# State space layer: one scan over two states from a zero start, the first token's state put into dt x B beforehand

## The chip, the cores and the metric

The kernel runs on one core of a Trainium2 chip. The core's engines work side by side, each through its own list of instructions in order: TensorE (PE; its weight loads are listed as PEld), VectorE (DVE), ScalarE (ACT), GpSimd (POOL), and SyncE (SP), which issues the DMAs. An instruction waits on semaphores until its inputs are there, and everything behind it on its engine waits with it. The metric is the device time of one execution in microseconds (us), smaller being better. All data is float32.

## The reference

Two layers, each added to its input: `x = x + L0(gn(x))`, then `x = x + L1(gn(x))`, on x of shape 4 x 384 x 64 x 64. L1 is attention over 7 x 7 windows and is the same in both kernels. L0 is a state space layer over the 4096 tokens of an image. For each of 768 inner channels d and 16 states n:

```python
dt  = softplus(dt_low @ dt_w.T + dt_b)      # per token and channel
A   = -exp(A_log)
def step(h, inp):
    dt_t, B_t, C_t, x_t = inp
    dA  = exp(dt_t[:, :, None] * A[None])
    dBx = (dt_t * x_t)[:, :, None] * B_t[:, None, :]
    h   = dA * h + dBx                        # the recurrence over tokens, h starts at 0
    y_t = einsum('bdn,bn->bd', h, C_t)
    return h, y_t
```

Around it: a group norm and a layer norm, an input projection to xb and a gate z, a causal convolution of 4 taps with SiLU on xb (the result is xc), the projections that give dt_low, B and C, and at the end `y + xc * D`, times SiLU(z), through the output projection.

## The kernel before, in words

Layer 0 runs in 64 steps: 4 images of 16 chunks of T = 256 tokens. The 768 channels are ND = 6 tiles d of 128 partitions. A tile's 16 states are four groups of NG = 4, so a step has 24 units m = 4 d + g. Each unit is worked in two slots, one for each half (two states), so that a step has 48 slots. What follows happens for one unit:

- `driven` (L595) makes db = (dt x) times B for four states in one instruction of 128 x 1024, on VectorE or on GpSimd. The table `AT['driven']` (L298) gives for each m its slot and a 1 for VectorE, 0 for GpSimd: before, 14 go to VectorE and 10 to GpSimd. VectorE reads dt x from a copy in PSUM (`dtx_ps`, copied by ScalarE in `dt_x_copied`, L592), GpSimd from SBUF. db has six buffers.
- `decay` (L605) makes da = exp(dt A) on ScalarE, one instruction of 128 x 256 for each state, into a PSUM tile of two states. Two of these tiles exist, so ScalarE can be one half ahead of VectorE: the decays of slot s + 1 are issued in slot s, and their tile comes free when the scans of slot s - 1 have ended.
- `scans` (L616) runs the recurrence on VectorE, one scan of 128 x 256 for each state, which starts from `state` (from 0.0 in the first chunk of an image). The result is hs, which has five buffers.
- `kept_states` (L629) copies the last token's states from hs into `state` on ScalarE, one copy of 128 x 4 for each unit, in the slot after the unit.
- `with_c` (L633) multiplies hs by C in place on GpSimd, one instruction of 128 x 1024 for each unit.
- `summed` (L637) adds the 16 states by transposing matmuls into PSUM (one buffer, `y`). For each pair of tiles d, `turn` (L654) copies that out on ScalarE, turns it back on TensorE and gates it on VectorE.

The order around this is written by hand. Every other piece of work has a slot in the table `AT` (L287), counted from the first slot of its step; negative slots lie in the step before and slots from 48 on in the step after. Within a slot, the ScalarE pieces come in this order: first decay, `kept_states` in even slots, second decay, and then the others; `with_c` and the scans follow, and then the other pieces on the other engines. The engines keep exactly this order. The pieces of one step that are prepared in the step before are the convolution and the projections (`prepared`, L425), whose `burst` (L479) runs all SiLUs between two loads of the activation table, the softplus (`softplus`, L514: three pairs of tiles, each a chain of projection, absolute value and relu, exp, plus one, ln, correction on VectorE, sum on TensorE, copy) and the layer norm (`normed`, L352). `rows` (L493) writes B and C to DRAM and reads each group of four states back into all 128 partitions, eight DMAs of 512 KB for each step on SP's queue; the four B tiles and four C tiles have one buffer for each group, which comes free when the last user in the step before has ended.

Layer 1 (from L821) starts when layer 0 has ended and isn't touched.

Of the kernel before, what the change touches and what calls it, by code (L numbers as in the profile page):

```python
# [8 lines left out]
F32 = mybir.dt.float32  # L9
# [39 lines left out]
def two_layers(  # L49
# [223 lines left out]
    def layer0(x1s, mvs, gms1):  # L273

        with ExitStack() as es:
            es.enter_context(tc.manual_schedule(engines=in_step))
            ps_a = es.enter_context(tc.tile_pool(name="ps_a", bufs=2, space=PSUM))
            ps_x = es.enter_context(tc.tile_pool(name="ps_x", bufs=1, space=PSUM))
# [8 lines left out]
            AT = {  # L287
             'norm': (9, 20, 21, 22, 22, 25, 28, 30, 32, 33, 33),
             'kept': -11,
             'x': ((-9, -8, -4, -4), (-6, -6, -3, -2), (-4, -4, -1, 1)),  # L290
             'c': ((1, 1, 5, 6), (3, 4, 8, 8), (8, 9, 13, 13)),
             'z': ((8, 9, 13, 13), (10, 11, 15, 15), (14, 15, 19, 21)),
             'burst': (25, 26, 28, 31),
             'softplus': ((32, 34, 36, 36, 37, 38, 40, 42), (34, 38, 39, 40, 42, 43, 44, 48),
                          (45, 49, 50, 50, 51, 51, 52, 55)),
             'dtx': (-5, -1, 8, 17, 19, 33),
             'dtx_ps': (-3, 4, 13, 20, 24, 36),
             'driven': ((-5, 0), (-2, 1), (-1, 1), (1, 1), (1, 0), (5, 1), (7, 0), (7, 1),  # L298
                        (11, 0), (14, 1), (14, 0), (16, 1), (19, 0), (21, 1), (23, 0), (25, 1),
                        (25, 1), (25, 1), (29, 0), (32, 1), (34, 0), (38, 1), (39, 0),  # L300
                        (41, 1)),
             'turn': (21, 25, 26),
             'out': (8, 17, 18, 19, 20, 22, 23, 27, 29, 30),
            }
            ACT = 1
            dtx_ps = ps_x.tile([P, 2, T], F32, name="dtx_ps")
            def group_norm(b, mv):
# [117 lines left out]
            def prepared(I, h, at):  # L425
# [67 lines left out]
                def rows():  # L493

                    xd = h["xd"] = w1.tile([NX, T], F32, tag="xd", name=f"xd_{b}_{i}")
                    nc.scalar.copy(xd, h["pd"][:NX, 0, :])
                    rows = dram.tile([2 * NS, T], F32, tag="bcrows", name=f"bcrows_{b}_{i}")
                    nc.sync.dma_start(rows, xd[DTR:NX, :])
                    h["B"], h["C"] = [], []
                    for tag in "BBBBCCCC":  # L500
                        g = len(h[tag])
                        t = bc.tile([P, NG, T], F32, tag=tag, name=f"{tag}_{b}_{i}_{g}")
                        r0 = g * NG + (NS if tag == "C" else 0)
                        src = rows[r0 : r0 + NG, :]
                        nc.sync.dma_start(t, src.unsqueeze(0).broadcast_to([P, NG, T]))
                        h[tag].append(t)
# [7 lines left out]
                def softplus(q, slots):  # L514
# [53 lines left out]
                    at(next(n), project)  # L568
                    s = next(n)
                    for k in range(2):  # L570
                        at(s, lambda k=k: part("e", AF.Abs, k), ACT)
                        at(s, lambda k=k: part("r", AF.Relu, k), ACT)
# [9 lines left out]

            dbs, das = {}, {}

# [7 lines left out]
            def dt_x_copied(d, h):  # L592
                nc.scalar.copy(dtx_ps[:, d % 2, :], h["dtx"][d])  # L593

            def driven(I, m, h, eng):  # L595

                d, g = divmod(m, NS // NG)
                db = w2.tile([P, NG, T], F32, tag="db", name=f"db_{I}_{m}", bufs=6)
                dtx = dtx_ps[:, d % 2, :] if eng is nc.vector else h["dtx"][d]
                eng.tensor_tensor(  # L600
                    db, dtx.unsqueeze(1).broadcast_to([P, NG, T]), h["B"][g], ALU.mult
                )
                dbs[I, m] = db

            def decay(I, m, half, k, h):  # L605

                d, g = divmod(m, NS // NG)
                n = g * NG + 2 * half + k
                if k == 0:
                    das[I, m, half] = ps_a.tile([P, 2, T], F32, tag="da", name="da")  # L610
                act(
                    das[I, m, half][:, k, :], h["dt"][d // 2][:, d % 2, :], AF.Exp,
                    scale=nega[:, d, n : n + 1],
                )

            def scans(I, m, half, hs):  # L616

                d, g = divmod(m, NS // NG)
                da = das.pop((I, m, half))
                for k in range(2):  # L620
                    j = 2 * half + k
                    n = g * NG + j
                    nc.vector.tensor_tensor_scan(  # L623
                        hs[:, j, :], da[:, k, :], dbs[I, m][:, j, :],
                        state[:, d, n : n + 1] if I % NCHUNK else 0.0,
                        ALU.mult, ALU.add,
                    )

# [117 lines left out]
            for I in range(STEPS):  # L746
# [7 lines left out]
                for d in range(ND):  # L754
                    at(AT["dtx"][d], lambda I=I, d=d, h=h: dt_x(I, d, h))
                    at(AT["dtx_ps"][d], lambda d=d, h=h: dt_x_copied(d, h), ACT)
                for m, (slot, vector) in enumerate(AT["driven"]):
                    eng = nc.vector if vector else nc.gpsimd
                    at(slot, lambda I=I, m=m, h=h, eng=eng: driven(I, m, h, eng))
                if I % NCHUNK == 0 and I + NCHUNK < STEPS:  # L760
                    next_batch(I // NCHUNK, slot_of(I))
# [461 lines left out]
```

## Time and profile before

| | us |
|---|---|
| median of 5 runs (8261.52 to 8269.91) | 8268.89 |
| profiled execution, its own time | 8266.53 |
| span of the profile | 8264.5 |
| layer 0, from the start to the last copy of states (5918.1) | 5918 |
| of it one step, from the copies of states (120.2 to 5918.1, 64 steps) | 90.65 |

Busy time between 1000 and 5000 us of the span, all inside layer 0:

| engine | busy, us of 4000 | us of one step of 90.65 |
|---|---|---|
| VectorE | 3767.8 | 85.4 |
| GpSimd | 3663.5 | 83.0 |
| TensorE | 3615.4 | 81.9 |
| ScalarE | 3245.9 | 73.6 |

The second column is the first divided by 4000 and multiplied by 90.65. Busy time counts a stretch in which two instructions of an engine overlap once. VectorE and ScalarE overlap the end of one instruction with the start of the next, so a row of many instructions takes less than their number times the mean of one; what an instruction adds to such a row is read from the timeline.

### The profile page before, as it was taken

The numbers are of one execution on the slowest core, as the hardware profiler recorded it, in microseconds if no ns is written. First come the engines' busy times: TensorE is split into PE (matmuls) and PEld (weight loads), VectorE is DVE, ScalarE is ACT, GpSimd is POOL, SyncE is SP. The second block draws the span as 40 slices with busy tenths as digits, with TensorE's granted clock in tenths as the row PEclk, the third lists the DMA queues.
The fourth block names the chain that finished last, engine by engine and source line by source line (L and its number), as shares of the span: only waits on it lengthen the run. The fifth ranks groups of instructions, "written<-read, shape, count | busy, mean of one in ns | idle before, by whom it ended". The sixth has DMA issues, their size and how long they took to land. (4 is left out here: it accounts for less than half of the span.)

```text
span 8264.5 us, 144369 instructions
## 1 busy us (share of the span) xinstructions
PE 7504.8 (91%) x48570; PEld 5811.4 (70%) x48570; DVE 6989.0 (85%) x12725; ACT 5890.5 (71%) x15613; POOL 6982.7 (84%) x4247
## 2 busy tenths in 40 slices
PE   7988998899899989988998999899799999999999
PEld 6777777777777777777777777777555555555555
DVE  5999999999999999999999999999666666666666
ACT  5888887888888887888878888888455455455455
POOL 4999998989999999999999999999677777677777
PEclk9999999999999999999999999999899999999999
DMA  3112211221121112112211211121223233232322
GB/s 111 62 61 72 70 59 59 67 67 60 64 76 62 55 62 75 60 64 73 66 53 59 66 60 55 60 71 51 80 84 87 85 89 88 82 88 84 89 82 64
DMA packets 327528, 583.40 MB, mean 71 GB/s; under 512 B 62940, under 2 KB 211180, under 8 KB 326660
## 3 DMA queue, kind: packets, MB, share of 16 engines
q1 hardware_dynamic: 326788, 574.17, 22.3%
q8 instruction: 387, 6.34, 0.3%
q14 instruction: 353, 2.89, 0.1%
HBM read 471.49 MB, written 84.73 MB: 67 GB/s over the span
## 5 line engine op out<-in xcount | busy, mean ns | idle before, releaser
L635 POOL TENSOR_TENSOR hs<-hs,C 128x1024 f32<-128x1024 f32 x1536 | 3615.8, 2362 | 468.9 <-ACT state L631 451.5
L623 DVE TENSOR_TENSOR_SCAN hs<-da,state,db 128x256 f32<-128x256 f32 x5760 | 3850.4, 730 | 121.1 <-issue 90.8
L96 ACT ACTIVATE da<-dt,nega 128x256 f32<-128x256 f32 x6144 | 2892.0, 475 | 885.1 <-DVE hs L623 839.7
L648 PE MATMUL y<-ident,hs 128*128 128x128 f32 x12288 | 1729.9, 293 | 596.6 <-POOL hs L635 355.2
L999 POOL TENSOR_SCALAR sg<-sg,rsum 128x308 f32<-128x308 f32 x1536 | 1618.8, 1072 | 641.7 <-DVE rsum L997 630.6
L648 PEld LDWEIGHTS y<-ident,hs 128*128 128x128 f32 x12288 | 1516.3, 151 | 892.7 <-POOL hs L635 518.3
L600 POOL TENSOR_TENSOR db<-dtx,B 128x1024 f32<-128x1024 f32 x640 | 1513.8, 2365 | 5.1
L409 PE MATMUL mm_ps<-xn,w_in 128*128 128x256 f32 x4608 | 1120.5, 390 | 2.0 <-DVE xn L380 1.9
L600 DVE TENSOR_TENSOR db<-dtx_ps,B 128x1024 f32<-128x1024 f32 x896 | 1065.6, 1201 | 0.7 <-ACT dtx_ps L593 0.7
L96 ACT ACTIVATE sg<-sg,mx 128x308 f32<-128x308 f32 x1536 | 828.6, 541 | 250.7 <-DVE mx L984 231.2
L984 DVE CUSTOM_DVE_ANT_0 sg<-lg_ps,bias 128x308 f32<-128x308 f32 x1536 | 643.1, 475 | 381.1 <-PE lg_ps L978 381.1
L409 PEld LDWEIGHTS mm_ps<-xn,w_in 128*128 128x128 f32 x4608 | 883.1, 198 | 114.9 <-DVE xn L380 2.7
L416 PE MATMUL mm_ps<-xb,dcv 128*128 128x256 f32 x3072 | 715.6, 379 | 0.0
L1027 ACT COPY tb<-pt_ps 88x512 f32<-88x512 f32 x384 | 221.8, 578 | 625.3 <-PE pt_ps L1023 625.2
L416 PEld LDWEIGHTS mm_ps<-xb,dcv 128*128 128x128 f32 x3072 | 571.7, 189 | 75.7 <-issue 0.3
L695 PE MATMUL mm_ps<-yg,w_out 128*128 128x256 f32 x2304 | 553.8, 381 | 0.0
L1014 DVE COPY ta<-pt_ps 110x512 f32<-110x512 f32 x768 | 492.5, 683 | 23.2 <-PE pt_ps L1009 23.2
L695 PEld LDWEIGHTS mm_ps<-yg,w_out 128*128 128x128 f32 x2304 | 437.1, 192 | 58.5
L1009 PE MATMUL pt_ps<-ident,sg 128*110 128x128 f32 x3072 | 417.7, 279 | 0.8 <-POOL sg L999 0.8
L1009 PEld LDWEIGHTS pt_ps<-ident,sg 128*110 128x110 f32 x3072 | 322.7, 133 | 77.9 <-issue 48.4
L882 PE MATMUL mm_ps<-xn,w_qkv 128*128 128x512 f32 (+2 forms) x612 | 278.0, 592 | 60.5 <-DVE xn L869 53.3
L978 PE MATMUL lg_ps<-k,q 32*128 32x308 f32 x3072 | 311.2, 473 | 0.0
(149 smaller groups left out, 10011.4 us busy)
## 6 DMA issues: line engine op xcount, KB each, us to landing
B<-bcrows SPq DMA_DIRECT2D x256, 512.0 KB
C<-bcrows SPq DMA_DIRECT2D x256, 512.0 KB
vw<-vd SPq DMA_DIRECT2D x1792, 33.0 KB
xr<-x SPq DMA_DIRECT2D x28, 1056.0 KB
vd<-v SPq DMA_DIRECT2D x280, 96.0 KB
xi<-in_x_dram SPq DMA_DIRECT2D x64, 384.0 KB
xo<-in_x_dram SPq DMA_DIRECT2D x64, 384.0 KB
x<-xo SPq DMA_DIRECT2D x64, 384.0 KB
```

Source lines behind the costliest of these rows:

```text
L96: ins = nc.scalar.activation(o, i, func, **kw)
L409: nc.tensor.matmul(pb[:, k, :], w_in[:, j, m * P : (m + 1) * P], xn[:, j, :], start=(j == 0), stop=(j == NJ - 1),)
L416: nc.tensor.matmul(pb[:, k, :], dcv[:, d, c, :], xb[:, d, c : c + T], start=(c == 0), stop=(c == KC - 1),)
L600: eng.tensor_tensor(db, dtx.unsqueeze(1).broadcast_to([P, NG, T]), h["B"][g], ALU.mult)
L623: nc.vector.tensor_tensor_scan(hs[:, j, :], da[:, k, :], dbs[I, m][:, j, :], state[:, d, n : n + 1] if I % NCHUNK else 0.0, ALU.mult, ALU.add,
L635: nc.gpsimd.tensor_tensor(hs, hs, h["C"][m % (NS // NG)], ALU.mult)
L648: nc.tensor.matmul(y[:, d % 2, half, :], hs[:, k, half * P : (half + 1) * P], ident, is_transpose=True, start=(first and half == 0 and d % ...
L695: nc.tensor.matmul(po, w_out[:, d, m * P : (m + 1) * P], h["yg"][d // 2][:, d % 2, :], start=False, stop=(d == ND - 1),)
L984: nc.vector.tensor_tensor_reduce(sg[:, hh, :], lg[:, :NK], bias[:, 4 * m + hh, :], -1.0, BIG, ALU.add, ALU.min, mx[:, hh : hh + 1],)
L999: nc.gpsimd.tensor_scalar(sg[:, hh, :], sg[:, hh, :], rs[:, hh : hh + 1], None, ALU.mult)
L1009: nc.tensor.transpose(pt[: KN[c], col : col + P], sg[:, 2 * pair + hh, KOFF[c] : KOFF[c] + KN[c]], ident,)
L1014: nc.vector.tensor_copy(t[: KN[0], :, :].rearrange("p a q -> p (a q)"), pt[: KN[0], :])
```

## The change

Two states are scanned by one instruction of 128 x 512 that starts from zero. At the border between the two, the decay is zero, which is how the second state begins afresh: the two PSUM tiles of decays are now fixed (`da_ps`), their first column of each state is set to zero once at the start, and `decay` writes only the other 255 columns. The state carried from the chunk before enters through db: its first column of each state gets the whole state of the first token, dA h + dBx. For that:

- a small DMA in `rows` brings the first token's B for 16 states into all 128 partitions (`B0`, 128 x 16);
- `start_decay` makes the first token's decays on ScalarE (six of 128 x 16 a step, none in the first chunk of an image);
- `first_states` makes the first token's states on GpSimd (a multiply by the first dt x, and, except in the first chunk, a multiply by the kept states and an add; 128 x 16 each, six tiles d);
- `begun` copies four of them into the first column of db on ScalarE (24 copies of 128 x 4 a step);
- `driven` writes the other 255 columns of each state. 16 of the 24 go to VectorE and 8 to GpSimd.

The table of slots is written anew throughout. Softplus has one more slot, so that its two pairs of absolute value and relu lie in slots of their own, and its third pair of tiles lies in slots 57 to 69, inside the step that uses it.

```diff
-            ps_a = es.enter_context(tc.tile_pool(name="ps_a", bufs=2, space=PSUM))
+            ps_a = es.enter_context(tc.tile_pool(name="ps_a", bufs=1, space=PSUM))
...
             AT = {
-             'norm': (9, 20, 21, 22, 22, 25, 28, 30, 32, 33, 33),
-             'kept': -11,
-             'x': ((-9, -8, -4, -4), (-6, -6, -3, -2), (-4, -4, -1, 1)),
-             'c': ((1, 1, 5, 6), (3, 4, 8, 8), (8, 9, 13, 13)),
-             'z': ((8, 9, 13, 13), (10, 11, 15, 15), (14, 15, 19, 21)),
-             'burst': (25, 26, 28, 31),
-             'softplus': ((32, 34, 36, 36, 37, 38, 40, 42), (34, 38, 39, 40, 42, 43, 44, 48),
-                          (45, 49, 50, 50, 51, 51, 52, 55)),
-             'dtx': (-5, -1, 8, 17, 19, 33),
-             'dtx_ps': (-3, 4, 13, 20, 24, 36),
-             'driven': ((-5, 0), (-2, 1), (-1, 1), (1, 1), (1, 0), (5, 1), (7, 0), (7, 1),
-                        (11, 0), (14, 1), (14, 0), (16, 1), (19, 0), (21, 1), (23, 0), (25, 1),
-                        (25, 1), (25, 1), (29, 0), (32, 1), (34, 0), (38, 1), (39, 0),
+             'norm': (11, 19, 19, 20, 20, 22, 26, 26, 30, 30, 32),
+             'kept': -15,
+             'x': ((-11, -11, -8, -7), (-11, -11, -7, -5), (-7, -6, -4, -3)),
+             'c': ((-3, -2, 0, 5), (3, 3, 7, 8), (15, 16, 18, 19)),
+             'z': ((1, 2, 3, 5), (10, 11, 14, 15), (8, 15, 16, 18)),
+             'burst': (25, 28, 28, 31),
+             'softplus': ((31, 33, 34, 36, 36, 37, 39, 39, 42),
+                          (44, 47, 47, 50, 50, 51, 52, 52, 55),
+                          (57, 60, 61, 61, 63, 65, 66, 66, 69)),
+             'dtx': (-5, -3, 9, 13, 23, 29),
+             'dtx_ps': (-3, 5, 10, 17, 24, 31),
+             'driven': ((-4, 0), (-3, 1), (-1, 1), (-1, 1), (1, 0), (6, 0), (6, 1), (8, 1),
+                        (10, 1), (11, 1), (14, 1), (15, 1), (18, 0), (19, 1), (23, 0), (25, 1),
+                        (25, 0), (26, 1), (30, 0), (32, 1), (35, 1), (36, 0), (36, 1),
                         (41, 1)),
-             'turn': (21, 25, 26),
-             'out': (8, 17, 18, 19, 20, 22, 23, 27, 29, 30),
+             'turn': (21, 24, 26),
+             'out': (11, 17, 21, 23, 23, 24, 26, 27, 29, 30),
+             'e0': (-4, -2, 11, 12, 23, 26),
+             'h0': (-4, -1, 11, 16, 24, 32),
+             'first': (-3, 0, 0, 4, 3, 7, 9, 10, 13, 14, 19, 18, 23, 23, 25, 27, 29, 30, 32, 33,
+                       38, 41, 41, 46),
             }
             ACT = 1
+            da_ps = [ps_a.tile([P, 2, T], F32, name=f"da_{half}") for half in range(2)]
+            for t in da_ps:
+                nc.vector.memset(t[:, :, 0:1], 0.0)
...
                     nc.sync.dma_start(rows, xd[DTR:NX, :])
+                    h["B0"] = small.tile([P, NS], F32, tag="b0", name=f"b0_{b}_{i}")
+                    with nc.allow_non_contiguous_dma(reason="one token"):
+                        nc.sync.dma_start(
+                            h["B0"],
+                            rows[:NS, 0:1].rearrange("n t -> t n").broadcast_to([P, NS]),
+                        )
...
                     at(next(n), project)
-                    s = next(n)
                     for k in range(2):
+                        s = next(n)
                         at(s, lambda k=k: part("e", AF.Abs, k), ACT)
                         at(s, lambda k=k: part("r", AF.Relu, k), ACT)
...
+            def start_decay(d, h):
+                h["e0", d] = w2.tile([P, NS], F32, tag="e0", name=f"e0_{d}", bufs=ND)
+                act(
+                    h["e0", d], nega[:, d, :], AF.Exp, scale=h["dt"][d // 2][:, d % 2, 0:1]
+                )
+
+            def first_states(I, d, h):
+                h["h0", d] = w2.tile([P, NS], F32, tag="h0", name=f"h0_{d}", bufs=ND)
+                dtx = h["dtx"][d][:, 0:1]
+                nc.gpsimd.tensor_scalar(h["h0", d], h["B0"], dtx, None, ALU.mult)
+                if I % NCHUNK:
+                    nc.gpsimd.tensor_tensor(h["e0", d], h["e0", d], state[:, d, :], ALU.mult)
+                    nc.gpsimd.tensor_tensor(h["h0", d], h["h0", d], h["e0", d], ALU.add)
+
+            def begun(I, m, h):
+                d, g = divmod(m, NS // NG)
+                nc.scalar.copy(dbs[I, m][:, :, 0], h["h0", d][:, g * NG : (g + 1) * NG])
...
                 eng.tensor_tensor(
-                    db, dtx.unsqueeze(1).broadcast_to([P, NG, T]), h["B"][g], ALU.mult
+                    db[:, :, 1:], dtx[:, 1:].unsqueeze(1).broadcast_to([P, NG, T - 1]),
+                    h["B"][g][:, :, 1:], ALU.mult,
                 )
...
-                if k == 0:
-                    das[I, m, half] = ps_a.tile([P, 2, T], F32, tag="da", name="da")
                 act(
-                    das[I, m, half][:, k, :], h["dt"][d // 2][:, d % 2, :], AF.Exp,
+                    da_ps[half][:, k, 1:], h["dt"][d // 2][:, d % 2, 1:], AF.Exp,
                     scale=nega[:, d, n : n + 1],
                 )
...
             def scans(I, m, half, hs):
-                d, g = divmod(m, NS // NG)
-                da = das.pop((I, m, half))
-                for k in range(2):
-                    j = 2 * half + k
-                    n = g * NG + j
-                    nc.vector.tensor_tensor_scan(
-                        hs[:, j, :], da[:, k, :], dbs[I, m][:, j, :],
-                        state[:, d, n : n + 1] if I % NCHUNK else 0.0,
-                        ALU.mult, ALU.add,
-                    )
+                pair = slice(2 * half, 2 * half + 2)
+                nc.vector.tensor_tensor_scan(
+                    hs[:, pair, :].rearrange("p k t -> p (k t)"),
+                    da_ps[half].rearrange("p k t -> p (k t)"),
+                    dbs[I, m][:, pair, :].rearrange("p k t -> p (k t)"),
+                    0.0, ALU.mult, ALU.add,
+                )
...
+                    if I % NCHUNK:
+                        at(AT["e0"][d], lambda d=d, h=h: start_decay(d, h), ACT)
+                    at(AT["h0"][d], lambda I=I, d=d, h=h: first_states(I, d, h))
                 for m, (slot, vector) in enumerate(AT["driven"]):
...
+                    at(AT["first"][m], lambda I=I, m=m, h=h: begun(I, m, h), ACT)
```

## The prediction

> **What bounds the kernel now.** I read the page first: its slices say where each engine is full, its groups what fills it.
>
> ```profile
> span 8264.5 us, 144369 instructions
> ...
> PE   7988998899899989988998999899799999999999
> ...
> DVE  5999999999999999999999999999666666666666
> ACT  5888887888888887888878888888455455455455
> POOL 4999998989999999999999999999677777677777
> ...
> L635 POOL TENSOR_TENSOR hs<-hs,C 128x1024 f32<-128x1024 f32 x1536 | 3615.8, 2362 | 468.9 <-ACT state L631 451.5
> L623 DVE TENSOR_TENSOR_SCAN hs<-da,state,db 128x256 f32<-128x256 f32 x5760 | 3850.4, 730 | 121.1 <-issue 90.8
> ```
>
> Slices 2 to 28 are layer 0; no slice there has an engine at rest. Then the busy time inside layer 0, by windows (length; busy and count of PE, PEld, DVE, ACT, POOL; clock, DMA):
>
> ```profile
> 1000.00:2000.00 1000.00, 904.88 (x4982) 769.52 (x4980) 942.09 (x1360) 809.63 (x2061) 914.23 (x449) 0.94 0.19 64
> 2000.00:3000.00 1000.00, 899.20 (x4974) 765.77 (x4974) 947.35 (x1356) 814.03 (x2071) 918.16 (x452) 0.94 0.20 64
> ```
>
> With the two windows that follow, a step of 90.65 us holds 85.4 us of VectorE, 83.0 of GpSimd, 81.9 of TensorE and 73.6 of ScalarE. VectorE is the bound, but GpSimd is 2.4 us and TensorE 3.5 us below it: what VectorE sheds beyond that another engine keeps. VectorE rests 5.2 us a step. The waits from 1000 to 5000 us, 44.1 steps, say for what:
>
> ```profile
> ACT da L96 <- DVE hs L623: 576.4, 785, 3.1
> ...
> POOL hs L635 <- ACT state L631: 316.8, 362, 3.9
> ...
> DVE yg L678 <- PE mm_ps L671: 115.1, 104, 2.9
> ...
> DVE hs L623 <- issue: 66.9, 89, 1.2
> ```
>
> VectorE waits 2.6 us a step for TensorE's gated sums and 1.5 with no releaser shown. ScalarE and GpSimd wait for VectorE's scans (13.1 and, through the kept states, 7.2 us). So VectorE sets the pace and the others follow it.
>
> **The change, part by part.** Durations are those of the profiled execution, 8266.53 us (2.4 us under the median of the five runs; span 8264.5).
>
> *Scans.* The timeline gives what one more scan costs in a row of them; the price of a moved product stands beside it.
>
> ```profile
> 130.47 8.54 DVE L623 TENSOR_TENSOR_SCAN hs<-da,db 128x256 f32<-128x256 f32 x14
> ...
> 2053.70 6.70 DVE L623 TENSOR_TENSOR_SCAN hs<-da,state,db 128x256 f32<-128x256 f32 x10
> ...
> 2066.59 3.46 DVE L600 TENSOR_TENSOR db<-dtx_ps,B 128x1024 f32<-128x1024 f32 x3
> ```
>
> From zero, one scan alone takes 0.671 us in its group and 14 take 8.54: (8.54 - 0.671)/13 = 0.605 each. From a kept state, (6.70 - 0.730)/9 = 0.663. No row has 512 columns. VectorE's statistics of 256 and 512 elements take 407 and 669 ns, so 145 ns of such an instruction don't depend on its length. Taken off the scan alone that leaves 0.526 us for 256 columns, and a scan of 512 in a row costs 0.605 + 0.526 = 1.13. [...]
>
> A pair from kept states goes from 1.326 to 1.13, 0.195 less, 9.4 us for 48 halves; in the 4 first chunks from 1.21 to 1.13, 3.8 us. Mean over 64 steps: 9.0 us less.
>
> *Products.* VectorE gets 16 instead of 14, each 1.13 us by the row of three above: 2.3 us more. GpSimd gets 8 instead of 10 at 2.33 us (2.365, less the overlap that rows of them show): 4.7 less. [...]
>
> VectorE: 85.4 - 9.0 + 2.3 = 78.7.
>
> *First token on GpSimd.* 18 instructions of 128 x 16 a step. Its product of 256 takes 731 ns and of 1024 2362 ns, which leaves 0.22 us for 16 elements; a fill of one element takes 0.1, the pad copy of 18 elements 0.2. So 1.8 to 4.5 us; I take 3.7. GpSimd: 83.0 - 4.7 + 3.7 = 82.0.
>
> *Copies and decays on ScalarE.* The copy of kept states has the shape of `begun`: 0.184 us alone, but in the timeline the next instruction starts 0.10 us after it.
>
> ```profile
> 2061.93 0.19 ACT L631 COPY state<-hs 128x4 f32<-128x4 f32 x1
> 2062.03 0.48 ACT L96 ACTIVATE da<-dt,nega 128x256 f32<-128x256 f32 x1
> ...
> 2066.43 1.28 ACT L96 ACT_TABLE_LOAD   x1
> 2067.72 1.67 ACT L96 ACTIVATE xc<-xc 128x512 f32<-128x512 f32 x3
> 2069.30 1.66 ACT L96 ACTIVATE sz<-sz 128x512 f32<-128x512 f32 x3
> 2070.97 1.28 ACT L100 ACT_TABLE_LOAD   x1
> ```
>
> 24 copies: 2.4 us, 4.4 at most. Six small exps at 0.2 (the exp of 32 x 1) to 0.28 (that of 128 x 96): 1.1 us after overlap. `kept_states` stays. ScalarE: 77.1, at most 79.7.
>
> *The B0 load.* One DMA of 2048 elements behind `bcrows` on SP, ahead of the B tiles. SP waits there anyway: 33 us a step for buffers that GpSimd and VectorE free (662.2, 509.7 and 277.1 us over 44 steps).
>
> ```profile
> SPq L505 <- POOL hs L635: 662.2, 176, 6.7
> SPq L505 <- POOL db L600: 509.7, 87, 10.0
> ...
> SPq L505 <- DVE db L600: 277.1, 87, 7.4
> ```
>
> In the step shown `bcrows` goes out at 2079.77 and the first B at 2090.34: 10 us of cover. Nearest row: the 25 loads of 784 runs of 28 bytes, issued in 16.06 us, 0.64 each; three times that is 1.7 us. I cost it nothing; without cover it would hold the first h0 by 2 us. [...] B's last tile has six slots from its last reader to its next instead of eight, still over 10 us. The fills of da_ps: once, 0.2 us.
>
> *Order.* Softplus lies in slots 31 to 69 instead of 32 to 55 and has the same instructions. Three places turn bad; each is the sum of what stands in a slot.
> - Burst, slots 25 and 26. ScalarE needs 0.8 (decays), then 5.84 (2066.43 to 2072.27), then 0.9 for the next decays: 7.6 us. VectorE had three products, a normalisation, two pairs of scans, gate and statistics to do meanwhile, 7.9 us. Now it has two scans, two products, gate and statistics: 5.4. It rests 2.2 us.
> - First unit, slots -4 and -3. `first_states` stands on GpSimd behind a `with_c` that starts 0.65 us after slot 44's start and takes 2.36; its copy on ScalarE is in slot 45, so the decays of slot 47, issued behind it, start 3.6 us (with 0.6 for h0) after the scan of slot 43 instead of 2.3 to 2.4: 1.2 us.
> - Slots 0 to 5. ScalarE: twelve decays at 0.41 (their distance in the timeline) 4.9, four copies of 256 columns with a bias 1.5, four steps of 512 columns 2.1, three copies of states, four of `begun` and one of dt x 1.0: 9.5. VectorE: six scans, a correction, half a statistic, 7.7, and 1.1 that it is behind from slot 47 (three and a half us of scan and products there, ScalarE 2.3). It rests 0.7 us.
>
> *Sum.* A step: 90.65 - 85.4 + 78.7 = 84.0 with the rest as today, + 2.2 + 1.2 + 0.7 = 88.1. 64 steps save 64 x 2.6 = 166 us: 8266.5 - 166 = **8100 us**. GpSimd would be busy 82.0 of 88.1, 93%, no more than VectorE is now (94%).
>
> **Rivals.**
> - *ScalarE held by `begun`: slower.* ScalarE runs in order, so a copy whose h0, or whose whole db, GpSimd still owes holds all decays behind it. For it: four copies follow within two slots a GpSimd product that stands behind a `with_c` (m = 0, 4, 5, 18), and ScalarE has 3.5 us a step less to give away. Against it: copy and product write different elements, so only h0 need be waited for, and h0 is early in five tiles of six. If the copy does wait for the product: first unit 3.6 instead of 1.2, m = 5 2.7 us, m = 4 and 18 some 1.4 each, 7.9 in all, some 5 after what VectorE has in hand: a step of 93, 64 x 2.35 = 150 more than before, 8417. It decides from 2.6 us a step on.
> - *The scan of 512 costs twice the 256: slower too.* VectorE sheds 5.2 us (5.6 in 60 steps of 64) instead of 9.0: a step of 91.9, 80 us more, 8347. Against it the fixed 145 ns.
> - *GpSimd takes the pace.* Its 82.0 plus the 7.2 it waits for states today is 89.2; 64 x 1.45 = 93 us less: 8174.
> - *No new stalls.* The spread softplus covers the three places. 84.0 would have GpSimd busy for 98%; at 96% it is 85.4: 8266.5 - 64 x 5.25 = 7930.
>
> **How the numbers follow.** My forecast 0.40, no new stalls 0.14, GpSimd's pace 0.12, held ScalarE 0.23, the dear scan 0.07, and 0.04 for a tie of gain and stalls. What a measurement here can tell from no change is 0.2%, 17 us. Faster 0.40 + 0.14 + 0.12 = 0.66, same 0.04, slower 0.30. The forecast's own range is 8020 to 8180. The whole range reaches down to 7910, just past the case without stalls, and up to 8400, short of the held ScalarE's 8417: about 0.07 lies below and 0.13 above.
>
> **What would show it.** Right: scans of 128 x 512 at about 1.2 us each; VectorE's share in layer 0 at 89 to 90% and its waits for ScalarE's da, now 18 us in 44 steps, above 100; GpSimd's wait for states smaller; nothing waiting for B0. Wrong: scans at 1.3 or more; long ScalarE waits for GpSimd's h0 or db; a GpSimd small operation above 0.3 us; TensorE waiting longer for GpSimd's hs (220.9 us in 44 steps now), which would keep hs buffers and stop the scans.

## The result, and the profile after

The changed kernel takes 8285.19 us (median), the kernel before 8267.61: a ratio of 1.0023, with a 95% interval of 1.0017 to 1.0028. It is a little slower. The forecast was 8100 us.

The page after shows the same slices and groups as before. VectorE's slices went from 9 to 8, and ScalarE's are at 8 without a gap.

```profile
span 8283.8 us, 144249 instructions
...
PE   6898999899989889998989899899799999999999
...
DVE  5888888888888888888888888888666666666666
ACT  4888888888888888888888888888555455455455
POOL 3999998989999898999989899999677777677777
...
L656 DVE TENSOR_TENSOR_SCAN hs<-da,db 128x512 f32<-128x512 f32 x3072 | 3622.8, 1211 | 355.7 <-ACT da L96 209.3
```

The scan of 512 takes 1.211 us and all scans together 3622.8 us instead of 4085.8 (3850.4 and the 235.4 of the first chunks). So VectorE did shed the work. The windows inside layer 0 (length; busy and count of PE, PEld, DVE, ACT, POOL; clock, DMA) say the same:

```profile
1000.00:2000.00 1000.00, 899.99 (x4968) 760.27 (x4966) 886.62 (x851) 839.72 (x2377) 905.23 (x613) 0.96 0.21 63
2000.00:3000.00 1000.00, 899.64 (x4965) 759.19 (x4962) 888.58 (x850) 844.35 (x2394) 912.63 (x627) 0.96 0.21 64
```

Copies of states now run from 128.3 to 5934.6 us, so a step takes 90.78 us instead of 90.65. The span is 19.3 us longer: 8.1 before the first copy of states, 8.4 in the steps, 2.8 after the last. In a step, from the four windows of 1000 to 5000 us (busy time over 4000, times the step):

| us a step | before | after | forecast |
|---|---|---|---|
| VectorE busy | 85.4 | 80.5 | 78.7 |
| GpSimd busy | 83.0 | 82.6 | 82.0 |
| TensorE busy | 81.9 | 81.7 | as before |
| ScalarE busy | 73.6 | 76.5 | 77.1 |
| VectorE waiting (step less busy) | 5.2 | 10.3 | 9.4 |
| step | 90.65 | 90.78 | 88.1 |

No engine works more than 91% of the step. VectorE's waits from 1000 to 5000 us, 44.1 steps (what waited, on whom, total, times, longest):

```profile
DVE hs L656 <- ACT da L96: 140.3, 215, 1.2
DVE yg L712 <- PE mm_ps L705: 135.0, 82, 2.6
DVE db L637 <- ACT dtx_ps L609: 69.0, 85, 1.1
DVE hs L656 <- ACT db L629: 67.2, 44, 1.7
DVE hs L656 <- POOL hs L669: 19.2, 47, 0.9
DVE hs L656 <- issue: 13.7, 3, 4.7
```

The wait for decays was 0.4 us a step before and is 3.2 now. The waits for copies into db (1.5) and for copies of dt x (1.6) are new. Where this comes from at the first unit is seen in the timeline (start, duration, then the instruction and in brackets the idle time before it):

```profile
2117.99 2.36 POOL L669 TENSOR_TENSOR hs<-hs,C 128x1024 f32<-128x1024 f32 x1 [1.43 <-ACT state L665]
...
2120.33 0.33 POOL L622 TENSOR_SCALAR h<-b,dtx 128x16 f32<-128x16 f32 x1
2120.62 0.22 POOL L624 TENSOR_TENSOR e<-e,state 128x16 f32<-128x16 f32 x1
2120.92 0.22 POOL L625 TENSOR_TENSOR h<-h,e 128x16 f32<-128x16 f32 x1
2121.10 2.35 POOL L637 TENSOR_TENSOR db<-dtx,B 128x1020 f32<-128x1020 f32 x1
2121.17 0.20 ACT L629 COPY db<-h 128x4 f32<-128x4 f32 x1 [0.75 <-POOL h L625]
...
2122.82 2.34 DVE L656 TENSOR_TENSOR_SCAN hs<-da,db 128x512 f32<-128x512 f32 x2 [1.55 <-ACT db L629]
```

GpSimd works on a multiplication by C from 2117.99. The three small operations stand behind it, ScalarE's copy behind them, the next decays and the last unit's copy behind that, and VectorE rests 1.55 us. The copy starts at 2121.17, while the product of the same unit runs until 2123.45: it waits for h0, the first token's states, alone.

### The profile page after: what moved, and what is told of

Same layout as the page of the kernel before. It is cut to its first block, busy times and chain, and to the rows that moved or that the text cites. A ratio compares the mean times of both kernels' runs of the same rounds, so it can differ in the third digit from the quotient of the medians.

```text
span 8283.8 us, 144249 instructions
## 1 busy us (share of the span) xinstructions
PE 7503.2 (91%) x48570; PEld 5772.0 (70%) x48570; DVE 6666.5 (80%) x9783; ACT 6076.5 (73%) x17509; POOL 6950.1 (84%) x5223
## 4 chain that ended last, share of the span: by engine, by line
PE 44%; ACT 21%; POOL 17%; DVE 12%; issue 5%; DMA 0%; SPq 0%; POOLq 0%; DVEq 0%; ACTq 0%
POOL hs L669 11%; ACT da L96 8%; DVE hs L656 6%; PE mm_ps L419 6%; PE y L682 5%; PE pt_ps L1047 4%; PE mm_ps L574 4%; PE mm_ps L426 3%; PE lg_ps L1016 3%; POOL db L637 3%; PE mm_ps L920 3%; PE mm_ps L1100 3%; PE mm_ps L953 3%; PE mm_ps L983 3%; PE pv_ps L1073 3%
## 5 line engine op out<-in xcount | busy, mean ns | idle before, releaser
L656 DVE TENSOR_TENSOR_SCAN hs<-da,db 128x512 f32<-128x512 f32 x3072 | 3622.8, 1211 | 355.7 <-ACT da L96 209.3
L96 ACT ACTIVATE da<-dt,nega 128x255 f32<-128x255 f32 x6144 | 2898.2, 474 | 700.3 <-DVE hs L656 673.7
L682 PE MATMUL y<-ident,hs 128*128 128x128 f32 x12288 | 1667.7, 283 | 466.3 <-POOL hs L669 449.0
L682 PEld LDWEIGHTS y<-ident,hs 128*128 128x128 f32 x12288 | 1443.7, 146 | 726.2 <-POOL hs L669 589.4
L637 DVE TENSOR_TENSOR db<-dtx_ps,B 128x1020 f32<-128x1020 f32 x1024 | 1223.3, 1200 | 111.5 <-ACT dtx_ps L609 106.6
L637 POOL TENSOR_TENSOR db<-dtx,B 128x1020 f32<-128x1020 f32 x512 | 1206.9, 2357 | 0.8 <-DMA B<-bcrows 0.8
L419 PE MATMUL mm_ps<-xn,w_in 128*128 128x256 f32 x4608 | 1164.1, 401 | 1.9 <-DVE xn L390 1.9
L419 PEld LDWEIGHTS mm_ps<-xn,w_in 128*128 128x128 f32 x4608 | 922.7, 206 | 133.2 <-DVE xn L390 2.3
L426 PE MATMUL mm_ps<-xb,dcv 128*128 128x256 f32 x3072 | 773.3, 400 | 9.3 <-DVE gm_b L270 9.3
L426 PEld LDWEIGHTS mm_ps<-xb,dcv 128*128 128x128 f32 x3072 | 591.9, 199 | 112.5 <-issue 19.9
```

The lines of the kernel that those rows point to most:

```text
L96: ins = nc.scalar.activation(o, i, func, **kw)
L419: nc.tensor.matmul(pb[:, k, :], w_in[:, j, m * P : (m + 1) * P], xn[:, j, :], start=(j == 0), stop=(j == NJ - 1),)
L426: nc.tensor.matmul(pb[:, k, :], dcv[:, d, c, :], xb[:, d, c : c + T], start=(c == 0), stop=(c == KC - 1),)
L637: eng.tensor_tensor(db[:, :, 1:], dtx[:, 1:].unsqueeze(1).broadcast_to([P, NG, T - 1]), h["B"][g][:, :, 1:], ALU.mult,)
L656: nc.vector.tensor_tensor_scan(hs[:, pair, :].rearrange("p k t -> p (k t)"), da_ps[half].rearrange("p k t -> p (k t)"), dbs[I, m][:, pair, ...
L682: nc.tensor.matmul(y[:, d % 2, half, :], hs[:, k, half * P : (half + 1) * P], ident, is_transpose=True, start=(first and half == 0 and d % ...
```

## The experiments

Three theories to begin with. First, VectorE's scans set the pace, and the added work took the gain back. Second, a chain through GpSimd, TensorE's list and VectorE's gate sets the step in both kernels. Third, the new table of slots costs. All runs are given as ratios to the kernel before, on the same chip. Not all ran on one chip, and the kernel before has medians from 8261.65 to 8269.09 us on them, so a difference in us between two runs is sure to some 8 us only. The columns "step", "VectorE" and "GpSimd" are us of one step, from the copies of states and the four windows of that run's profile.

**The parts one at a time.** `scan_only`: the kernel before, with the scan of two states.

```diff
+            da_ps = [ps_a.tile([P, 2, T], F32, name=f"da_{half}") for half in range(2)]
+            for t in da_ps:
+                nc.vector.memset(t[:, :, 0:1], 0.0)
...
-                for k in range(2):
...
-                        hs[:, j, :], da[:, k, :], dbs[I, m][:, j, :],
-                        state[:, d, n : n + 1] if I % NCHUNK else 0.0,
...
+                    hs[:, pair, :].rearrange("p k t -> p (k t)"),
+                    da_ps[half].rearrange("p k t -> p (k t)"),
+                    dbs[I, m][:, pair, :].rearrange("p k t -> p (k t)"),
+                    0.0, ALU.mult, ALU.add,
```

> The kernel before, its table of slots and its 14 and 10 products, with one scan of two states from zero, and nothing else: no state is carried from one chunk of 256 tokens to the next (the kept states are still copied, but not read). It leaves out B0, start_decay, first_states and begun. Theory 1, VectorE's scans set the pace and the added work took the gain back: VectorE falls from 85.4 to 78 us a step, GpSimd (83.0) and TensorE (81.9) become the floor, a step of 85 to 87 and 7900 to 8030 us. Theory 2, a chain that runs through GpSimd, TensorE's list and VectorE's gate sets the step in both kernels, and VectorE's scans are only a part of it: 8180 us or more, with VectorE's waits grown by what its scans shed.

`new_no_carry`: the changed kernel without what carries states.

```diff
-                    at(AT["h0"][d], lambda I=I, d=d, h=h: first_states(I, d, h))
-                    at(AT["first"][m], lambda I=I, m=m, h=h: begun(I, m, h), ACT)
...
-                    db[:, :, 1:], dtx[:, 1:].unsqueeze(1).broadcast_to([P, NG, T - 1]),
-                    h["B"][g][:, :, 1:], ALU.mult,
+                    db, dtx.unsqueeze(1).broadcast_to([P, NG, T]), h["B"][g], ALU.mult
```

> The changed kernel with its table of slots, without what carries the states: no B0, no start_decay, no first_states, no begun, and dt x B written over all 256 columns; every chunk starts from zero. GpSimd is 4.3 us a step shorter, ScalarE some 4. Theory 1: the added work cost the gain, so this is well under before, 7950 to 8080 us. Theory 2, the chain: GpSimd's share of the chain shrinks by the small operations that lie on it (1.3 of some 90 us at two places), so 8150 to 8250 us. Theory 3, the new table of slots is what costs: 8230 us or more.

`old_table_new_scan`: the whole new scheme in the old table, all other entries of AT being those of the kernel before.

```diff
+             'e0': (-5, -1, 6, 14, 17, 30),
+             'h0': (-5, -1, 8, 17, 19, 33),
+             'first': (-3, 0, 1, 4, 4, 8, 10, 10, 14, 16, 18, 20, 22, 24, 26, 28, 29, 31, 33, 35,
+                       38, 40, 42, 44),
```

> The whole new scheme, exact, in the table of slots of the kernel before (softplus and the 14 and 10 products too), with slots for the first states two to five slots ahead of their scans. GpSimd then has 10 products and 18 small operations, 87 us a step. Theory 1: added work sets the time, 8300 us or more, GpSimd being the bound at 87 plus waits. Theory 2: the same, since GpSimd is on the chain. Theory 3, the new table is what costs: under 8250 us.

`new_table_old_scan`: the kernel before, with all entries of AT of the changed kernel that it has a use for, and softplus's extra slot; two of them:

```diff
-             'dtx': (-5, -1, 8, 17, 19, 33),
+             'dtx': (-5, -3, 9, 13, 23, 29),
...
-             'turn': (21, 25, 26),
+             'turn': (21, 24, 26),
```

> The kernel before, one scan for each state from its kept state, in the new table of slots (16 and 8 products, softplus spread). VectorE holds 87.8 us a step. Theory 1, VectorE's time sets the pace of a step: some 2.4 us a step more than before, 8420 us or more. Theory 2, the chain: GpSimd is 4.7 us shorter than before, and VectorE as the bound with few waits gives 90 to 92 us a step, 8230 to 8340. Theory 3, the new table costs by itself: above 8450 us.

| run | us | ratio, 95% interval | step | VectorE | GpSimd |
|---|---|---|---|---|---|
| scan_only | 8177.55 | 0.9893 (0.9878 to 0.9908) | 89.01 | 78.7 | 82.9 |
| new_no_carry | 8151.74 | 0.9864 (0.9849 to 0.9879) | 88.69 | 80.3 | 78.7 |
| old_table_new_scan | 8456.93 | 1.0233 (1.0216 to 1.025) | 93.45 | 78.9 | 87.0 |
| new_table_old_scan | 8330.90 | 1.0080 (1.0065 to 1.0095) | 91.57 | 87.4 | 78.7 |

`scan_only` decides the first half of the first theory, and against it. VectorE sheds 6.7 us a step with nothing added, and the step falls by 1.64: a quarter. The rest is in its waits from 1000 to 5000 us, first the three smaller ones of the kernel before (44.1 steps; the prediction shows the two large ones), then those of `scan_only` (44.9 steps):

```profile
DVE hs L623 <- ACT da L96: 18.3, 52, 1.3
DVE spe L548 <- ACT dt L96: 17.4, 44, 0.8
DVE xn L380 <- PE mm_ps L374: 8.5, 7, 1.8
...
DVE yg L677 <- PE mm_ps L670: 214.4, 132, 3.0
DVE hs L621 <- issue: 111.6, 116, 1.7
DVE hs L621 <- ACT da L96: 50.0, 125, 2.0
DVE spe L551 <- ACT dt L96: 34.0, 45, 0.9
DVE xn L383 <- PE mm_ps L377: 25.2, 41, 2.1
```

The wait for the gated sums went from 2.6 to 4.8 us a step, that without a releaser from 1.5 to 2.5, and the other three, 1.0 together before, make 2.4. So most of VectorE's time was not what held the kernel before, though it was 94% busy. In the new table the same change of scans (`new_table_old_scan` to `new_no_carry`) is worth more, 2.9 us of step and 179 us in all for 7.1 us of VectorE. Along that path the total adds up: the table with its two moved products +67 us, the scans -179, the carrying +133, in all 21 where 18 were measured. So the second half of the first theory holds as a sum: table and carrying together take the scans' gain back. The third theory does not explain the loss. The table costs 67 us under the old scans, but the new scheme in the old table takes 8457, with 10 products and 18 small operations on GpSimd, busy 87.0.

Of the four expectations, three came out at the second theory's figures or within 3 us of them, against the first's; `old_table_new_scan` fits the first and the second alike.

**What of the carrying costs 133 us, and is TensorE on the path?** `new_short_conv` and `old_short_conv` take time off TensorE alone, in each kernel.

```diff
-                for c in range(KC):
+                for c in range(2, KC):
```

> The changed kernel with two of the four taps of the causal convolution left out, which takes some 6 us a step off TensorE and off no other engine. If TensorE's list is on the chain that sets the step, as the chain of the changed kernel shows (its matmuls have some 30% of it), half or more of that comes back: 8090 us or less. If GpSimd sets it, or ScalarE and VectorE holding each other, TensorE's time is cover: within 60 us of 8285.

> The kernel before with the same two taps left out, some 6 us a step off TensorE. If VectorE's 85.4 of 90.65 us set the pace of before, as the prediction had it, TensorE's time is worth only the waits for the gated sums, 2.6 us a step: 8100 to 8240 us, and not under. If a chain through TensorE sets it there too: under 8100.

`new_no_first_states` leaves the copies and takes GpSimd's part away; `first_states_on_vector` gives that part to VectorE.

```diff
-                nc.gpsimd.tensor_scalar(h["h0", d], h["B0"], dtx, None, ALU.mult)
...
+                h["h0", d] = no_states
```

> The changed kernel without the 18 small operations on GpSimd (4.4 us a step): the 24 copies on ScalarE stay and read a constant, the B0 load and the six small exps stay; no state is carried. Without all of the carrying it was 8152. If GpSimd's operations cost the 133 us: 8150 to 8190. If ScalarE's copies and exps do: 8250 to 8290. Halves: about 8220.

```diff
-                nc.gpsimd.tensor_scalar(h["h0", d], h["B0"], dtx, None, ALU.mult)
...
+                nc.vector.tensor_tensor(h["e0", d], h["e0", d], state[:, d, :], ALU.mult)
+                nc.vector.scalar_tensor_tensor(h["h0", d], h["B0"], dtx, h["e0", d], ALU.mult, ALU.add)
```

> The changed kernel, exact, with the first states made on VectorE by two instructions of 128 x 16 for each of six tiles instead of three on GpSimd: 4.4 us a step off GpSimd, some 1.5 to 2 on to VectorE, which rests 10 us a step. If GpSimd's operations are what the carrying costs and VectorE's idle time is to be had: 8170 to 8210, under the kernel before. If a step is set by VectorE's and ScalarE's waits for each other, VectorE's addition counts in full: 8285 or more.

| run | us | ratio, 95% interval | step |
|---|---|---|---|
| new_short_conv | 8276.49 | 1.0014 (1.0004 to 1.0023) | 90.74 |
| old_short_conv | 8254.19 | 0.9986 (0.9977 to 0.9995) | 90.50 |
| new_no_first_states | 8188.94 | 0.9904 (0.9889 to 0.9919) | 89.30 |
| first_states_on_vector | 8715.52 | 1.0541 (1.0524 to 1.0559) | 97.47 |

TensorE became 3.9 to 4.2 us a step shorter (77.8 and 77.7) and the time fell by some 10 us in each kernel, where the second theory expected 8090 us or less and under 8100. The second theory falls in this form: the chain of the changed kernel names TensorE's lines for a quarter, but taking work out of one of them (L426, the convolution) shortened next to nothing. That would be so if the same end is reached by another way as well; which way was not shown. The chain's shares by line between 1000 and 5000 us, first part:

```profile
by line: POOL hs L669 15.3%; ACT da L96 11.9%; DVE hs L656 9.0%; PE mm_ps L419 7.8%; PE y L682 7.4%; issue 6.3%; PE mm_ps L574 4.9%; POOL db L637 4.6%; PE mm_ps L426 4.6%; DVE db L637 3.8%; ACT xc L96 2.8%; ACT sz L96 2.7%; POOL dtx L603 2.
```

GpSimd's small operations have 96 of the 133 us. That looked like GpSimd's time, 4.1 us of it; the next runs say otherwise. On VectorE two small operations for each tile cost 430 us. The groups of that run, from 1000 to 5000 us:

```profile
L623 DVE TENSOR_TENSOR e<-e,state 128x16 f32<-128x16 f32 x227 | 276.3, 1217 | 6.2 <-ACT e L96 6.2
L624 DVE SCALAR_TENSOR_TENSOR h<-b,dtx,e 128x16 f32<-128x16 f32 x227 | 276.0, 1216 | 24.0 <-DVE e L623 0.9
```

1.2 us for 16 columns. The last section shows when they take so long.

**GpSimd's time, or its place?** Three edits of the changed kernel, which all compute the same as it does.

```diff
-                        (25, 0), (26, 1), (30, 0), (32, 1), (35, 1), (36, 0), (36, 1),
+                        (25, 1), (26, 1), (30, 0), (32, 1), (35, 1), (36, 0), (36, 1),
```

> The changed kernel, exact, with the product of unit 16 moved from GpSimd to VectorE in the same slot 25, the one of the SiLU burst, where VectorE waits about 2 us for ScalarE: 2.3 us a step off GpSimd, 1.1 on to VectorE into that rest. If GpSimd's time counts as it did for the first states (96 us for 4.4): about 50 us less, 8235. If VectorE's time counts as well (179 us for 7 us): 28 of it given back, 8262. If the waits at the burst set the step: more than 8285.

```diff
-                nc.gpsimd.tensor_scalar(h["h0", d], h["B0"], dtx, None, ALU.mult)
+                act(h["h0", d], h["B0"], AF.Identity, scale=h["dtx"][d][:, 0:1])
-             'h0': (-4, -1, 11, 16, 24, 32),
+             'h0': (-4, 0, 11, 16, 24, 32),
+             'p0': (-4, 0, 11, 15, 24, 31),
```

> The changed kernel, exact, with the first of the three small operations for each tile (B0 times the first dt x) made by ScalarE: 6 x 0.33 = 2.0 us a step off GpSimd, some 1.2 on to ScalarE. If GpSimd's time counts and ScalarE's little: about 8250. If ScalarE in its order counts as much: 8285 or more.

```diff
-             'dtx': (-5, -3, 9, 13, 23, 29),
+             'dtx': (-6, -3, 8, 13, 23, 29),
-             'e0': (-4, -2, 11, 12, 23, 26),
-             'h0': (-4, -1, 11, 16, 24, 32),
+             'e0': (-6, -2, 11, 12, 23, 26),
+             'h0': (-6, -1, 11, 16, 24, 32),
```

> The changed kernel, exact, nothing moved between engines: dt x of tile 0 and its first states go two slots ahead on GpSimd, in front of a multiplication by C (slot -6), and dt x of tile 2 one slot ahead. ScalarE's waits for them, 1.4 and 0.9 us a step, and VectorE's behind them (1.5 for the first unit's copy, about half of 1.6 for the copies of dt x) should go. If such single waits lie on what sets the step: 1 to 2 us a step, 8150 to 8220. If they only stand in for another wait: 8260 to 8290.

`new_all_three` has all of them, but the multiplication of tile 0 then stands on ScalarE at slot -5, and GpSimd's two operations come after it, at -4 again.

> The three edits together, exact. If they add up, the sum of the three differences, some 8100 to 8200 and faster than the kernel before. If the waits stand in for each other, no more than the best of the three.

| run | us | ratio, 95% interval | step | GpSimd |
|---|---|---|---|---|
| new_one_product_moved | 8276.87 | 1.0015 (1.0005 to 1.0024) | 90.74 | 80.3 |
| new_one_multiply_on_scalar | 8270.26 | 1.0006 (0.9997 to 1.0016) | 90.56 | 80.8 |
| new_earlier_products | 8187.79 | 0.9907 (0.9892 to 0.9922) | 89.35 | 82.6 |
| new_all_three | 8276.16 | 1.0013 (1.0004 to 1.0023) | 90.74 | 78.4 |

This is the clearest result. 2.3 and 1.8 us a step off GpSimd gave 8 and 15 us. In these two runs another engine took the work on (VectorE 1.1 us a step more, ScalarE 1.3), so alone they don't show that GpSimd's time is free. `new_earlier_products` does. Moving the first states of tile 0 and its dt x ahead of one multiplication by C, with GpSimd as busy as before, gave 97, as much as taking all 18 small operations away (8187.79 and 8188.94 us, with GpSimd busy 82.6 and 78.5 us a step). So the 4.1 us of GpSimd's time are cover here, hidden behind other waits; one tile's lateness cost 1.4 us a step. The edit also moved tile 0's small exp, which `new_no_first_states` leaves where it was, and dt x of tile 2, which changed nothing in VectorE's wait for the copies of dt x (69.0 us before, 68.2 after). The timeline of `new_earlier_products` shows the place mended:

```profile
2087.89 0.33 POOL L622 TENSOR_SCALAR h<-b,dtx 128x16 f32<-128x16 f32 x1
2088.18 0.22 POOL L624 TENSOR_TENSOR e<-e,state 128x16 f32<-128x16 f32 x1
...
2088.48 0.22 POOL L625 TENSOR_TENSOR h<-h,e 128x16 f32<-128x16 f32 x1
...
2088.91 2.36 POOL L669 TENSOR_TENSOR hs<-hs,C 128x1024 f32<-128x1024 f32 x1 [0.20 <-ACT state L665]
...
2091.32 0.18 ACT L629 COPY db<-h 128x4 f32<-128x4 f32 x1
...
2092.96 2.34 DVE L656 TENSOR_TENSOR_SCAN hs<-da,db 128x512 f32<-128x512 f32 x2 [0.73 <-ACT db L629]
```

h0 is ready at 2088.7, ScalarE's copy no longer waits, and VectorE's wait is 0.73 instead of 1.55. With all three edits h0 was late again (VectorE's wait at this place is 1.54 us) and the gain was gone, which agrees. That run is less clear, because ScalarE there also waits 1.54 us for dt x of tile 0.

**Does every wait count in full?** Built on `new_earlier_products`, each run on the one named in its expectation.

```diff
-             'dtx': (-6, -3, 8, 13, 23, 29),
+             'dtx': (-6, -3, 7, 13, 23, 29),
```

> The changed kernel, exact, with the first unit's work at slot -6 as in the run with earlier products, and dt x of tile 2 at slot 7, ahead of the multiplication by C of slot 8; at slot 8 it still stood behind it, and ScalarE's wait of 1.39 us for it and VectorE's of 1.13 behind that were unchanged. If places count in full: 64 x 1.1 = 70 us less than 8188, 8118. If waits stand in for each other: 8170 to 8190.

`new_burst_eased`, built on it:

```diff
-             'norm': (11, 19, 19, 20, 20, 22, 26, 26, 30, 30, 32),
+             'norm': (11, 19, 19, 20, 20, 22, 28, 28, 30, 30, 32),
-             'e0': (-6, -2, 11, 12, 23, 26),
+             'e0': (-6, -2, 11, 12, 23, 24),
```

> The run before in this list with the square of the layer norm and its sum two slots later (28) and the first decay of tile 5 two slots earlier (24), so that slot 26 holds only decays and kept states on ScalarE behind the burst: VectorE's second wait there, 1.05 us, should go, the first, 1.07, stay. If places count in full: 64 x 1.0 = 64 us less than the run before. If not: within 20 us of it.

`new_eased_product_moved` moves unit 16's product as above, on that:

> The run before in this list with the product of unit 16 moved from GpSimd to VectorE in slot 25, before the wait of 1.07 us at the burst: GpSimd 2.3 us a step less, VectorE 1.1 more. If GpSimd's time counts now that the places are mended: 50 us less. If only VectorE's work and its waits count, the product fills the wait: within 20 us of the run before.

`new_gate_later`, built on `new_tile2_ahead`; `new_ahead_product_moved` moves unit 16's product on that same kernel:

```diff
-             'turn': (21, 24, 26),
+             'turn': (21, 24, 28),
```

> The run with tile 2 ahead, with VectorE's gate two slots later (28 instead of 26), so that TensorE has two more slots for the turn back; VectorE's wait for it, 132 us in 45 steps or 2.9 us a step, should go. If it lies on what sets the step: 64 x 2 to 2.9 us, 7985 to 8045. If it stands in for others (ScalarE's decays, TensorE's own list): 8130 to 8171.

> The run with tile 2 ahead, with the product of unit 16 on VectorE in slot 25: GpSimd, busy 93% of a step there, sheds 2.3 us, VectorE gets 1.1 in front of its waits at the burst. If GpSimd sets the step at 93%: 50 us less. If its time is cover: within 20 us of 8171.

| run | us | ratio, 95% interval | step |
|---|---|---|---|
| new_tile2_ahead | 8170.96 | 0.9886 (0.9869 to 0.9902) | 89.04 |
| new_burst_eased | 8241.79 | 0.9967 (0.9956 to 0.9979) | 90.23 |
| new_eased_product_moved | 8251.35 | 0.9979 (0.9970 to 0.9989) | 90.28 |
| new_gate_later | 8173.96 | 0.9891 (0.9876 to 0.9905) | 89.20 |
| new_ahead_product_moved | 8179.09 | 0.9897 (0.9881 to 0.9914) | 89.14 |

They don't. Tile 2's dt x took VectorE's wait for the copies of dt x from 68.2 to 24.1 us, and gained 17 us instead of 70: the wait for the gated sums grew from 100.0 to 132.1. Gating later took that wait out of the list altogether and gained nothing; VectorE then waits longer for decays (162.4 before that edit) and for dt x. First two lines of `new_earlier_products` (44.8 steps), then two of `new_tile2_ahead` (44.9), then two of `new_gate_later` (44.8):

```profile
DVE yg L712 <- PE mm_ps L705: 100.0, 84, 2.6
DVE db L637 <- ACT dtx_ps L609: 68.2, 85, 1.1
...
DVE yg L712 <- PE mm_ps L705: 132.1, 87, 2.4
...
DVE db L637 <- ACT dtx_ps L609: 24.1, 45, 0.5
...
DVE hs L656 <- ACT da L96: 260.1, 220, 3.5
DVE db L637 <- ACT dtx_ps L609: 82.5, 90, 1.9
```

Easing the burst lost 71 us. The sum of squares now stands later in TensorE's list, behind the projection of the SiLU's output, and ScalarE waits 3.3 us a step for it, a wait that `new_tile2_ahead` doesn't have:

```profile
ACT mm_ps L96 <- PE mm_ps L384: 145.8, 44, 5.3
```

A product off GpSimd changed nothing in either run (8 and 10 us up), though GpSimd is busy for 93% of the step in `new_tile2_ahead`. Of the versions that carry the states, that one is the fastest, 1.1% under the kernel before; `new_gate_later` is the same within the intervals.

## Why the prediction was wrong

- **The scan.** Right: alone 1.211 us (forecast 1.20), in a row (3.49 - 1.211)/2 = 1.14 from a row of three (forecast 1.13). But most scans now stand alone or in pairs, so the prices in long rows were too low: by the groups of layer 0 the scans shed 7.2 us a step, not 9.0, and two more products cost 2.5, not 2.3. That makes 2.0 us; the windows show 1.8 (80.5 instead of 78.7). A product of 255 columns for each state takes VectorE 1.200 us where one of 256 took 1.201, and GpSimd 2.357 where it took 2.365. VectorE's products, before and after:

```profile
L600 DVE TENSOR_TENSOR db<-dtx_ps,B 128x1024 f32<-128x1024 f32 x896 | 1065.6, 1201 | 0.7 <-ACT dtx_ps L593 0.7
...
L637 DVE TENSOR_TENSOR db<-dtx_ps,B 128x1020 f32<-128x1020 f32 x1024 | 1223.3, 1200 | 111.5 <-ACT dtx_ps L609 106.6
```

- **GpSimd and ScalarE.** Right to 0.6 us each. The multiply with a pointer takes 0.33 us where 0.2 was put in, the other two 0.22.
- **The B0 load.** Right: no engine waits for it, and SP issues it in 0.37 us (median of 64). **begun waiting for the whole product.** It doesn't: the first unit's copy, at 2121.17, starts 2.28 us before that product's end.
- **The three places.** As waits of VectorE, right in place and size: at the burst 1.07 and 1.05 us (forecast 2.2 together), at the first unit 1.55 (1.2), in slots 0 to 5 0.65 (0.7). Not foreseen: two waits for copies of dt x, 1.6 us a step, the longer of them, 1.12, behind GpSimd's dt x of tile 2, which stands behind a multiplication by C in the same manner. What such a wait is worth is another matter: the first unit's was worth 1.4 us of the step, tile 2's 0.3.

```profile
2077.74 3.49 DVE L656 TENSOR_TENSOR_SCAN hs<-da,db 128x512 f32<-128x512 f32 x3
...
2088.07 1.22 DVE L656 TENSOR_TENSOR_SCAN hs<-da,db 128x512 f32<-128x512 f32 x1 [1.07 <-ACT da L96]
2090.35 3.67 DVE L656 TENSOR_TENSOR_SCAN hs<-da,db 128x512 f32<-128x512 f32 x3 [1.05 <-ACT da L96]
...
2133.16 1.22 DVE L656 TENSOR_TENSOR_SCAN hs<-da,db 128x512 f32<-128x512 f32 x1 [0.65 <-ACT da L96]
...
2145.62 1.22 DVE L637 TENSOR_TENSOR db<-dtx_ps,B 128x1020 f32<-128x1020 f32 x1 [1.12 <-ACT dtx_ps L609]
```

- **The sum: this step failed.** "84.0 with the rest as today" let VectorE's shed time come off the step in full, with its waits of 5.2 us unchanged. `scan_only` has the forecast's 78.7 us of VectorE with nothing added, and its step is 89.0, not 84: three quarters turned into waits, most of all for the gated sums. The three places were then added to a base that wasn't there. From the measured base without carrying (`new_no_carry`, 88.7), the copies and exps add 0.6 (`new_no_first_states`, 89.3) and the first unit's lateness 1.4, which is the step of 90.7 to 90.8.
- **The same miss, read off the changed kernel alone.** There 1.8 of the 2.7 us by which the step missed stand in VectorE's busy time and 0.9 in its waits, as if the price of the scans had failed. But the runs put VectorE's time at a quarter (old table) to two fifths (new table) of itself, so the 1.8 us are worth some 0.4 to 0.7 of the step, an estimate from these two. That the waits came out near the forecast, 10.3 for 9.4, is partly luck: those of the old kinds (gated sums, no releaser, the 0.4 of decays) fell from 5.2 to 3.8, and the new ones make 6.3 instead of 4.1.
- **The rivals.** Two of them said slower, and it is a little slower, but not by their mechanism. The held ScalarE's 5 us a step needed copies that wait for the whole product, which they don't; what held ScalarE is h0 of the first unit, which the forecast itself had priced at 1.2 us. The scan of 512 is not dear: 1.211 us, under twice the 0.671 of 256. GpSimd's pace falls with the runs in which its time was cover, and "no new stalls" with the three places.
- **Its own signs.** VectorE's share is 89% and its waits for da are 140.3 us, as the forecast wanted. GpSimd's wait for states hardly fell, from 316.8 to 306.0. Two signs of being wrong appeared: a small operation of 0.33 us, and TensorE's wait for GpSimd's hs, 285.1 us instead of 220.9.
- **VectorE "sets the pace and the others follow it".** The waits of the others for scans were read as proof, with VectorE at 94%. But GpSimd at 92% and TensorE at 90% were in nearly the same position, and in `scan_only` what VectorE gave up went to other waits.

Open: what sets the 89 us that remain. In `new_tile2_ahead` no engine is over 93%, and 2.3 us off GpSimd gained nothing; in the kernels before and after, 4 us off TensorE was worth 10 us of the whole time; and waits of VectorE's that were removed came back at other places. A chain that passes through several lists in order would do that, but which one it is was not shown.

## What to carry to other kernels

Where several engines are 80 to 94% busy and each follows a fixed order, the busiest one's time need not be the price of the step (here 6.7 us a step off VectorE were worth 1.64): measure what its shed work is worth with nothing else added before summing. An instruction's place in a slow engine's list can be worth more than its length (here tile 0's place 1.4 us a step, with GpSimd as busy as before): look for a small result that another engine's list must wait for, and put it ahead of the long instruction. And cost an operation by the rows it will stand in after the change, not by the longest rows that stand there now (a scan of 512 took 1.211 us alone, 1.14 in a row of three).

## What the runs showed of the hardware

In `first_states_on_vector` VectorE's small operations, all of whose inputs are in SBUF, last until the end of GpSimd's running multiplication by C or product where they start during one. The multiply of 128 x 16 takes from 0.148 to 2.326 us, its median 1.349. The timeline:

```profile
2006.86 0.15 DVE L623 TENSOR_TENSOR e<-e,state 128x16 f32<-128x16 f32 x1
...
2007.70 2.34 POOL L672 TENSOR_TENSOR hs<-hs,C 128x1024 f32<-128x1024 f32 x1 [1.23 <-ACT state L668]
...
2015.48 2.35 POOL L672 TENSOR_TENSOR hs<-hs,C 128x1024 f32<-128x1024 f32 x1 [0.69 <-DVE db L640]
2016.54 1.33 DVE L623 TENSOR_TENSOR e<-e,state 128x16 f32<-128x16 f32 x1
...
2030.19 2.36 POOL L640 TENSOR_TENSOR db<-dtx,B 128x1020 f32<-128x1020 f32 x1
2030.42 2.15 DVE L623 TENSOR_TENSOR e<-e,state 128x16 f32<-128x16 f32 x1
```

At 2006.86 GpSimd rests and the multiply takes 0.15 us. The other two end at 2017.87 and 2032.57, within 0.05 us of the end of GpSimd's instruction (2017.83 and 2032.55). These three are no exceptions. From 1000 to 5000 us, all 264 of the small operations (L623 and L624) that start while GpSimd works on a multiplication by C or a product end 0.02 to 0.05 us after it; the other 190 start while GpSimd rests and take 0.15 to 0.24 us. VectorE's scans and products read one operand from PSUM and show no such times: in the same run all scans take 1.158 to 1.226 us and all products 1.181 to 1.222. The price was up to almost the whole length of GpSimd's instruction (a multiply of 2.33 us beside 2.36). Why they end together was not shown.
